# Where a column sum is taken: the mean row of a graph-attention kernel from GpSimd's running sum, adj's buffers on multiples of 512 bytes, and two-input comparisons

## The chip, the cores and the metric

The kernel runs on one core of a Trainium2 chip. The metric is the time of one execution on the device in microseconds; "the time" of a kernel is the median of its runs. A core has five engines with a queue of instructions each: TensorE (PE; its weight loads are listed as PEld), VectorE (DVE), ScalarE (ACT), GpSimd (POOL) and SyncE (SP), which here only issues transfers. ACT and POOL issue transfers too. Sixteen DMA engines carry them out. A wait between engines is a wait on a semaphore. The on-chip memory has 128 partitions; a tile of [128, n] has n elements in each.

## The reference, cut to what matters

Two layers over a graph of N = 4096 nodes with 512 features; about one entry of adj in a thousand is 1, some four neighbours a node. The first layer is attention over the neighbours with eight heads of 64, the second a mean over the neighbours with two dense products. Each is added to its input and normalised.

```python
Wh = jnp.einsum('nf,hfo->hno', x, W)
f1 = jnp.einsum('hno,ho->hn', Wh, a[:, :F_OUT])
f2 = jnp.einsum('hno,ho->hn', Wh, a[:, F_OUT:])
e = jax.nn.leaky_relu(f1[:, :, None] + f2[:, None, :], ALPHA)
e = jnp.where(adj[None, :, :] > 0, e, NEG_INF)
attn = jax.nn.softmax(e, axis=-1)
out = jnp.einsum('hnm,hmo->hno', attn, Wh)
...
mask = (adj > 0).astype(x.dtype)
agg = mask @ x / jnp.maximum(jnp.sum(mask, axis=1, keepdims=True), 1.0)
combined = jnp.concatenate([x @ W_self + b_self, agg @ W_nb + b_nb], axis=-1)
out = jax.nn.relu(combined @ W_comb + b_comb)
...
x = _layernorm(x + out, axis=-1)
```

A node without neighbours has all its scores at the same value, so its softmax is flat, and its row of `out` is the mean of all rows of Wh. This is the "mean row" of the kernel: one row, the average over 4096 nodes.

## The kernel before

The kernel does not multiply by the dense mask. It turns adj into short lists of neighbours and gathers rows by index.

**The adjacency loop** (b = 0 to 26, to about 202 us). Nodes are handled in 32 blocks of 128. For each block of adj, `load_adj` (line 427, SP's queue) brings two halves of 1 MB into the tiles `at` (four buffers); `mask_adj` (L433, ACT) turns a half into bf16 `ab` (three buffers) and counts it; `fold_adj` (L452, PE) packs the mask into key values in PSUM; `max_keys` (L467, DVE) takes the largest keys of a row; and once in four blocks `decode` (L469 to 566, DVE with a few small matmuls) makes the lists of neighbours. It is a generator: the loop takes a few steps of it per block. Two comparisons of `decode`, `va` (L500) and `ni` (L509), work on small tiles; a third, `lt` (L535), is a 128x128 tile for each block, followed by a two-input instruction (L536) that finishes the 0/1 matrix. `late_lists` has the same pair (L594, L595). Blocks 28 to 31 of adj come later, in the attention stage.

In the same loop every node block of x is loaded (`load_x`, SP), transposed on PE (`transposed`, L353) and copied from PSUM to the tile xT by ACT, and then multiplied with the weights: `node_half`, 8 matmuls of 128x264 (L369), whose result of 528 columns DVE copies to a tile `row` (L373, three buffers). The 528 columns are 8 scores f2, 512 of Wh and 8 scores f1. `node_rest` (L396 to L398) copies the scores away on GpSimd, and `store` (L974) writes the row block to the table t0 in HBM, from GpSimd's queue, except for the last block (w = 31), whose store is SP's.

**The mean row** is made from x: the mean of Wh's rows is the mean of x's rows times the weights. For most blocks the copy to xT is done in four pieces with an accumulator each (L361), which sums the columns of x; for four early blocks ACT copies (L356) and DVE reduces (L358). After the loop `mean_row` reduces the sums (L405, L406), multiplies them with the weights `w_sb` (L412, 16 matmuls with one column of weights), copies the result (L416) and stores it as row N + 2 of t0 (L417, ACT's queue).

**After the loop** the order is written by hand. SP issues the last block's store, then the loads of `wr` and `wc` (1 MB each) and two late pieces of adj into `m` (`load_late`). Then comes the first gather, `gather(t0, 0, ...)`: five indirect transfers per block (`rows_of`, L631, GpSimd's queue), four of rows that are shared by several nodes (k = 1 to 4, over the first N + 2 rows) and one over the whole table (k = 0). Its buffer `g` has five copies, `GA` = 5. The first lies where `w_sb` and the sums had been, the others where `at`, `colf`, `ab` and the like had been; so each waits for the last reader of those. Then the folds of adj's blocks 26 and 27 (LB - 1 and LB) and the last decode, the product of W_nb and W_comb (`fold_weights`, PE and ACT), and the attention stage proper (L681 to L755), which runs to about 530 us. The second layer follows.

All tiles are laid out in memory in the order in which they are asked for, so a tile's size moves those behind it. Some tiles ask for more than they use for that reason (`wc` for 8 columns more, `ni` for 8 instead of 4).

Of the kernel before, what the change touches and what calls it, by code (L numbers as in the profile page):

```python
# [31 lines left out]
F32 = mybir.dt.float32  # L32
# [3 lines left out]
AF = mybir.ActivationFunctionType  # L36
OP = mybir.AluOpType
# [3 lines left out]
P = 128  # L41
# [19 lines left out]
G = 4  # L61
# [52 lines left out]
def listed_layers(  # L114
# [207 lines left out]
    def bias_columns(brw):  # L322

        bt = ps.tile([P, 2 * FB], F32, name="sm", bufs=2)
        nc.tensor.transpose(bt, brw, ident[0 : 2 * FB, 0 : 2 * FB])
        bcol = small.tile([P, 2 * FB], F32, name="bcol", bufs=1)
        nc.scalar.copy(bcol, bt)
        return bcol
# [19 lines left out]

    def transposed(b, wp, sums=None):

        tp = ps.tile([P, FB, P], F32, name="tp", bufs=1)
        for c in range(FB):
            nc.tensor.transpose(tp[:, c, :], xs[:, b, ts(c, P)], ident)  # L353
        t = wp.tile([P, FB, P], F32, name="xT", bufs=4)
        if sums is None or b % 2 == 0 and b < XL:
            nc.scalar.copy(t, tp)  # L356
            if sums is not None:
                nc.vector.tensor_reduce(sums[:, :, b : b + 1], tp, AX.X, OP.add)  # L358
        else:
            for c in range(FB):  # L360
                nc.scalar.activation(  # L361
                    t[:, c, :], tp[:, c, :], AF.Copy, accum_out=sums[:, c, b : b + 1]
                )
        return t
# [36 lines left out]

    def mean_row(w_sb, sums, wp):

        xm = small.tile([P, FB], F32, name="xm", bufs=1)
        nc.vector.tensor_reduce(xm, sums, AX.X, OP.add)  # L405
        nc.vector.tensor_scalar(xm, xm, 1.0 / N, None, OP.mult)  # L406
        mr = wp.tile([P, FW], F32, name="row", bufs=3)
        for k in range(2):
            r = slice(k * HW, (k + 1) * HW)
            pq = ps.tile([1, HW], F32, name="sm", bufs=2)  # L410
            for c in range(FB):
                nc.tensor.matmul(  # L412
                    pq, lhsT=xm[:, c : c + 1], rhs=w_sb[:, c, r],
                    start=(c == 0), stop=(c == FB - 1),
                )
            nc.vector.tensor_copy(mr[0:1, r], pq)  # L416
        nc.scalar.dma_start(t0[N + 2 : N + 3, :], mr[0:1, :])  # L417
# [51 lines left out]
    def decode(b0, dp, place):  # L469
# [24 lines left out]
        for g in range(G):  # L494
# [4 lines left out]
        va = dp.tile([P, G, KL], F32, name="va", bufs=1)  # L499
        nc.vector.tensor_scalar(va, nb, float(SHIFT), None, OP.is_ge)  # L500
        nc.vector.tensor_reduce(deg[:, bs], va, AX.X, OP.add)
# [3 lines left out]
        )  # L505
        ni = dp.tile([P, 8], F32, name="ni", bufs=1)[:, 0 : G * K0].rearrange(
            "p (g k) -> p g k", g=G
        )
        nc.vector.tensor_scalar(ni, L[:, :, 0:K0], 0.0, float(N + 2), OP.is_equal, OP.mult)  # L509
# [21 lines left out]
        for b in range(b0, b0 + G):  # L531
            io, off, en = iota[:, 0:P], lst[:, b, KL : KL + 1], end[:, b : b + 1]
            lt = dp.tile([P, P], F32, name="lt", bufs=1)
            st = place(b)
            nc.vector.tensor_scalar(lt, io, en, None, OP.is_lt)  # L535
            nc.vector.scalar_tensor_tensor(st, io, off, lt, OP.is_ge, OP.mult)  # L536
            sts.append(st)
            yield
# [31 lines left out]
    def late_lists(dp, place):  # L570
# [21 lines left out]
        for b in range(NE):  # L592
            lt = dp.tile([P, P], F32, name="lt", bufs=1)
            nc.vector.tensor_scalar(lt, iota[:, 0:P], endl[:, b : b + 1], None, OP.is_lt)  # L594
            nc.vector.scalar_tensor_tensor(  # L595
                place[:, b, :], iota[:, 0:P], tl[:, b, KL : KL + 1], lt, OP.is_ge, OP.mult
            )
            if b % 2:
                yield
# [227 lines left out]
    def weight(pool, name):  # L827
        w = pool.tile([P, FB * HD + (8 if name == "wc" else 0)], F32, name=name)
        return w[:, 0 : FB * HD].rearrange("p (c o) -> p c o", c=FB)
# [7 lines left out]
    bp = bp_cm.__enter__()  # L837
    colf = bp.tile([P, SC], F32, name="colf")
    nc.gpsimd.iota(
        colf, [[1, SC]], base=0, channel_multiplier=0, allow_small_or_imprecise_dtypes=True  # L840
# [28 lines left out]
    nc.scalar.dma_start(brow[0:1, :], b_comb.rearrange("(a o) -> a o", a=1))  # L869
    sums = xa.tile([P, FB, NB], F32, name="sums")  # L870
    pa = []
# [3 lines left out]
    nc.scalar.copy(av[:, 0], pa[0])  # L875
    xT = transposed(0, wp, sums)

# [29 lines left out]
    def node_block(w, xT, between=None, keep=False, then=lambda: None):  # L907
# [11 lines left out]
        if not keep:  # L919
            store(w, row, nc.gpsimd)  # L920
        return row

# [54 lines left out]
    for b in range(LB):  # L977
# [6 lines left out]
        for k in range(2):  # L984
            some(lists)
        ahead = [transposed(w + 1, wp, sums) if w + 1 < NB else None]
        key_bank(b + 1)
        mask_adj(b + 1, 0)

        def then():  # L990
            ahead.append(transposed(w + 2, wp, sums))
            mask_adj(b + 1, 1)
# [21 lines left out]
    loaded = load_fold(1, w_nb, m2, weight(fc, "wc"))  # L1014
    mean_row(w_sb, sums, wp)
    for k in range(2):
# [13 lines left out]
    m2s = fold_weights(loaded, place, "pw")  # L1030
    fold_adj(LB - 1, dp)
    max_keys(LB - 1)
    for k in range(4):
# [588 lines left out]
```

## Time and profile before

| | |
|---|---|
| median of 7 runs | 774.17 us (760.61 to 784.87) |
| the profiled execution | 770.34 us, of which the span from the first to the last instruction is 768.6 us |
| mean granted TensorE clock of the profiled execution | 0.906 |
| instructions | 9452 |
| busy: PE, DVE, ACT, POOL | 599.4, 409.3, 410.6, 353.5 us |
| moved by DMA | 210.46 MB, 274 GB/s over the span |
| the adjacency loop | to about 202 us |
| the attention stage | about 212 to 530 us |
| the second layer | about 530 to 768 us |

The profile is one execution on the chip. A row of a group gives the line, the engine, the operation, the tile written and the tiles read, the shapes and the count; then the busy time, the mean duration of one, and the idle time of the engine just before them with what ended most of it. A timeline's row gives start, duration, engine, line, operation and, in brackets, the idle time before it and its releaser. A "queue" (SPq, ACTq, POOLq) is the issuing of transfers, not the transfer.

### The profile page before, as it was taken

Reading aid. Unit: us, or ns where it says so; the run is one execution under the profiler, and the core shown is the slowest. Engines: PE = TensorE matmul, PEld = TensorE weight load, DVE = VectorE, ACT = ScalarE, POOL = GpSimd, SP = SyncE. Lnnn points to the kernel's source line nnn. Section 1 sums busy time; section 2 is a strip of 40 time slices with the busy share of each in tenths; the row PEclk is TensorE's granted clock in tenths of the full one; section 3 lists DMA queues with packets and bytes.
Section 4 is the critical chain, followed back from the end, with each engine's and each line's share of the span. In section 5 each row is a group of like instructions: output and inputs, shape, how many; then the busy total and the mean of one; then the engine's idle time right before and its main releaser. Section 6 shows DMA issues by size and latency. Waiting matters only on the chain.

```text
span 768.6 us, 9452 instructions
## 1 busy us (share of the span) xinstructions
PE 599.4 (78%) x2569; PEld 294.4 (38%) x2570; DVE 409.3 (53%) x1182; ACT 410.6 (53%) x1087; POOL 353.5 (46%) x472
## 2 busy tenths in 40 slices
PE   6888888899735697669686676868959987888794
PEld 4666666676412343223232232323413322222231
DVE  6246686978573667557675764652024233323342
ACT  3587878888511386566464454444234444434353
POOL 4111211121175456555565564645736666666620
PEclk9799999999867799888798898979989998998998
DMA  8999999999976679887786687658758877787752
GB/s 265 391 374 380 393 395 393 393 394 391 368 219 170 196 273 388 293 249 242 294 237 224 213 243 244 202 183 271 210 180 249 270 237 252 238 269 255 237 204 74
DMA packets 92108, 210.46 MB, mean 274 GB/s; under 512 B 13761, under 2 KB 13769, under 8 KB 92048
## 3 DMA queue, kind: packets, MB, share of 16 engines
q1 hardware_dynamic: 63296, 114.32, 41.2%
q0 software_dynamic: 28560, 95.17, 40.0%
q8 instruction: 23, 0.38, 0.2%
q10 hardware_dynamic: 192, 0.28, 0.1%
q14 instruction: 37, 0.30, 0.1%
HBM read 175.91 MB, written 33.83 MB: 273 GB/s over the span
## 4 chain that ended last, share of the span: by engine, by line
PE 33%; DMA 19%; issue 15%; ACT 12%; another core or an unknown queue 12%; DVE 7%; SPq 1%; ACTq 0%; DVEq 0%
DMA at<-in_adj_dram 18%; PE pw L776 7%; PE nm L776 6%; PE pw L750 6%; ACT ab L433 3%; PE num L706 3%; PE pw L369 3%; PE nm L783 2%; PE pw L783 2%; PE pw L314 1%; ACT xs L736 1%; ACT xs L745 1%; ACT xT L356 1%; PE sm L412 1%
## 5 line engine op out<-in xcount | busy, mean ns | idle before, releaser
L631 POOL DMA_INDIRECT g<-t,idx x290 | 275.5, 950 | 191.4 <-issue 80.3
L750 PE MATMUL pw<-wr,xT 128*128 128x512 f32 x256 | 130.8, 657 | 0.7 <-ACT xT L356 0.7
L433 ACT ACTIVATE ab<-at 128x2048 bf16<-128x2048 int32 x56 | 107.2, 1915 | 41.4 <-DMA at<-in_adj_dram 32.4
L369 PE MATMUL pw<-w_sb,xT 128*128 128x264 f32 x496 | 124.9, 400 | 4.0 <-DVE row L393 2.0
L369 PEld LDWEIGHTS pw<-w_sb,xT 128*128 128x128 f32 x496 | 92.6, 195 | 27.8 <-issue 3.7
L706 PE MATMUL num<-g,own 128*32 128x256 f32 (+1 forms) x512 | 43.0, 463 | 69.4 <-ACT num L699 52.2
L396 POOL COPY lst<-row 128x8 f32<-128x8 f32 x32 | 6.9, 216 | 154.8 <-DVE row L373 118.8
L750 PEld LDWEIGHTS pw<-wr,xT 128*128 128x128 f32 x256 | 51.1, 211 | 70.0 <-issue 64.2
L681 DVE TENSOR_TENSOR g<-g,ew 128x2048 f32<-128x2048 f32 x32 | 73.1, 2284 | 0.0
L776 PE MATMUL pw<-m,xT 128*128 128x512 f32 x128 | 63.1, 620 | 6.6 <-issue 6.2
L776 PE MATMUL nm<-m,xT 128*128 128x512 f32 x128 | 64.3, 643 | 2.7 <-issue 2.7
L714 DVE RECIPROCAL rd<-num 128x8 f32<-128x8 f32 x32 | 6.6, 207 | 93.1 <-PE num L706 21.7
L671 ACT ACTIVATE ew<-e 128x40 f32<-128x40 f32 x32 | 6.6, 207 | 85.8 <-issue 43.6
L706 PEld LDWEIGHTS num<-g,own 128*32 128x32 f32 x512 | 15.0, 122 | 86.8 <-ACT num L699 57.8
L373 DVE COPY row<-pw 128x264 f32<-128x264 f32 x62 | 26.5, 428 | 38.0 <-PE pw L369 31.3
L353 PE MATMUL tp<-ident,xs 128*128 128x128 f32 x256 | 40.4, 282 | 6.9 <-issue 2.0
L754 ACT COPY row<-pw 128x512 f32<-128x512 f32 x32 | 18.7, 584 | 47.9 <-PE pw L750 22.4
L353 PEld LDWEIGHTS tp<-ident,xs 128*128 128x128 f32 x256 | 31.6, 145 | 30.6 <-issue 18.7
L799 DVE SCALAR_TENSOR_TENSOR sm<-g,lst,pw 128x512 f32<-128x512 f32 x15 | 11.3, 754 | 59.1 <-remote 32.3
L799 DVE SCALAR_TENSOR_TENSOR sm<-g,lst,nm 128x512 f32<-128x512 f32 x15 | 11.3, 753 | 59.1 <-PE nm L783 39.2
L776 PEld LDWEIGHTS nm<-m,xT 128*128 128x128 f32 x128 | 25.0, 204 | 42.5 <-issue 38.4
L776 PEld LDWEIGHTS pw<-m,xT 128*128 128x128 f32 x128 | 23.5, 194 | 46.3 <-issue 42.6
(234 smaller groups left out, 964.2 us busy)
## 6 DMA issues: line engine op xcount, KB each, us to landing
at<-in_adj_dram SPq DMA_DIRECT2D x56, 1024.0 KB
xt<-xT SPq DMA_DIRECT2D x32, 256.0 KB
t<-row SPq DMA_DIRECT2D x32, 256.0 KB
xT<-xt SPq DMA_DIRECT2D x32, 256.0 KB
out_dram<-row SPq DMA_DIRECT2D x32, 256.0 KB
t<-row POOLq DMA_DIRECT2D x31, 264.0 KB
xs<-in_x_dram SPq DMA_DIRECT2D x31, 256.0 KB
m<-in_adj_dram SPq DMA_DIRECT2D x10, 512.0 KB
```

The costliest lines, as they stand in the source:

```text
L353: nc.tensor.transpose(tp[:, c, :], xs[:, b, ts(c, P)], ident)
L369: nc.tensor.matmul(pw, lhsT=xT[:, c, :], rhs=w_sb[:, c, k * HW : (k + 1) * HW], start=(c == 0), stop=(c == FB - 1),)
L373: nc.vector.tensor_copy(row[:, k * HW : (k + 1) * HW], pw)
L433: nc.scalar.activation(ab, loads.pop((b, h)), AF.Relu, accum_out=asum[:, b, h : h + 1])
L631: nc.gpsimd.indirect_dma_start(out=out, out_offset=None, in_=table, in_offset=bass.IndirectOffsetOnAxis(ap=at, axis=0),)
L681: nc.vector.tensor_tensor(gv, gv, E[b][:, sl].unsqueeze(3).to_broadcast([P, sl.stop - sl.start, H, D]), OP.mult,)
L706: nc.tensor.matmul(NM[b][ts(k, HP), a * HD : a * HD + r.stop - r.start], lhsT=OWN[b][:, k, :], rhs=G0[b][:, K0 + k, r], start=False, stop= ...
L750: nc.tensor.matmul(pz, lhsT=xT[:, c, :], rhs=m2[:, c, :], start=(c == 0), stop=(c == FB - 1))
L754: nc.scalar.copy(z[:, 0:HD], pz)
L776: nc.tensor.matmul(NM[b], lhsT=xT[:, c, :], rhs=m1[:, c, :], start=False, stop=(c == FB - 1), skip_group_check=True,)
L783: nc.tensor.matmul(NM[b][ts(k, HP), :], lhsT=OWN[b][:, k, :], rhs=g[:, K0 + k, 0:HD], start=False, stop=True, tile_position=(0, k * HP), s ...
L799: nc.vector.scalar_tensor_tensor(yp, Y[b], lst[:, b, KL + 1 : KL + 2], NM[b], OP.mult, OP.add)
```

## The change

Four things change.

1. The sums over x go. `transposed` copies to xT with one ACT instruction for every block, and DVE reduces nothing. In their place `add_row` lets GpSimd keep a running sum `acc` of the rows of Wh: a copy for block 0, then an addition of [128, 528] for blocks 1 to 30, each queued behind that block's store. `mean_row` multiplies `acc` and the last block's `row` by a column of 1/N (`inv_n`) and so sums over the partitions: four matmuls with one column of weights instead of 16.
2. The fold of adj's block 26 and its maxima move ahead of the mean row; before, they stood behind it. The order on PE is then: eight fold matmuls, four of the mean row; on DVE: four maxima, then the two copies of the mean row. ACT's and SP's orders stay as they are.
3. Sizes: `bcol` 16 columns instead of 8, `acc` new with 640, `wc` without its 8 further columns, `xm`, `sums` and `ni` gone (`ni` uses the buffer of `jx`). In the built program the four buffers of `at` start at 141312, 149504, 157696 and 165888 bytes within a partition, multiples of 512; before, they started at 143808, 152000, 160192 and 168384, each 448 past a multiple. `colf`, `acc`, `ab` and the first tiles of `decode` start on multiples of 512 too.
4. The comparisons `va` and `lt` become two-input instructions: compare, then multiply with a tile of ones.

The diff, without repetitions:

```diff
...
         bt = ps.tile([P, 2 * FB], F32, name="sm", bufs=2)
         nc.tensor.transpose(bt, brw, ident[0 : 2 * FB, 0 : 2 * FB])
-        bcol = small.tile([P, 2 * FB], F32, name="bcol", bufs=1)
+        bcol = small.tile([P, 4 * FB], F32, name="bcol", bufs=1)[:, 0 : 2 * FB]
         nc.scalar.copy(bcol, bt)
         return bcol
...
         if b < NB:
             eng.dma_start(xs[:, b, :], x[ts(b, P), :])
-    def transposed(b, wp, sums=None):
+    def transposed(b, wp):
         tp = ps.tile([P, FB, P], F32, name="tp", bufs=1)
         for c in range(FB):
             nc.tensor.transpose(tp[:, c, :], xs[:, b, ts(c, P)], ident)
         t = wp.tile([P, FB, P], F32, name="xT", bufs=4)
-        if sums is None or b % 2 == 0 and b < XL:
-            nc.scalar.copy(t, tp)
-            if sums is not None:
-                nc.vector.tensor_reduce(sums[:, :, b : b + 1], tp, AX.X, OP.add)
-        else:
-            for c in range(FB):
-                nc.scalar.activation(
-                    t[:, c, :], tp[:, c, :], AF.Copy, accum_out=sums[:, c, b : b + 1]
-                )
+        nc.scalar.copy(t, tp)
         return t
     def node_half(b, k, xT, w_sb, row):
...
             f1s[:, b, 0:K0, :], row[:, TW:FW].unsqueeze(1).to_broadcast([P, K0, H])
         )
-    def mean_row(w_sb, sums, wp):
-
-        xm = small.tile([P, FB], F32, name="xm", bufs=1)
-        nc.vector.tensor_reduce(xm, sums, AX.X, OP.add)
-        nc.vector.tensor_scalar(xm, xm, 1.0 / N, None, OP.mult)
+    def add_row(b, row):
+        if b == 0:
+            nc.gpsimd.tensor_copy(acc, row)
+        else:
+            nc.gpsimd.tensor_tensor(acc, acc, row, OP.add)
+
+    def mean_row(row, wp):
+
         mr = wp.tile([P, FW], F32, name="row", bufs=3)
         for k in range(2):
             r = slice(k * HW, (k + 1) * HW)
             pq = ps.tile([1, HW], F32, name="sm", bufs=2)
-            for c in range(FB):
-                nc.tensor.matmul(
-                    pq, lhsT=xm[:, c : c + 1], rhs=w_sb[:, c, r],
-                    start=(c == 0), stop=(c == FB - 1),
-                )
+            for n, t in enumerate((acc, row)):
+                nc.tensor.matmul(pq, lhsT=inv_n, rhs=t[:, r], start=(n == 0), stop=(n == 1))
             nc.vector.tensor_copy(mr[0:1, r], pq)
         nc.scalar.dma_start(t0[N + 2 : N + 3, :], mr[0:1, :])
...
             nc.vector.max(nb[:, g, 8:16], kj[:, g, :])
             yield
         va = dp.tile([P, G, KL], F32, name="va", bufs=1)
-        nc.vector.tensor_scalar(va, nb, float(SHIFT), None, OP.is_ge)
+        nc.vector.scalar_tensor_tensor(
+            va, nb, float(SHIFT), ones[:, 0 : G * KL].rearrange("p (g k) -> p g k", g=G),
+            OP.is_ge, OP.mult,
+        )
         nc.vector.tensor_reduce(deg[:, bs], va, AX.X, OP.add)
         L = lst[:, bs, :]
         nc.vector.scalar_tensor_tensor(
             L[:, :, 0:KL], nb, float(2 - SHIFT), va, OP.add, OP.mult
         )
-        ni = dp.tile([P, 8], F32, name="ni", bufs=1)[:, 0 : G * K0].rearrange(
-            "p (g k) -> p g k", g=G
-        )
+        ni = dp.tile([P, G, KH], F32, name="jx", bufs=1)[:, :, 0:K0]
         nc.vector.tensor_scalar(ni, L[:, :, 0:K0], 0.0, float(N + 2), OP.is_equal, OP.mult)
         nc.vector.scalar_tensor_tensor(
             idx[:, bs, 0:K0], L[:, :, 0:K0], float(N + 1), ni, OP.min, OP.max
...
             io, off, en = iota[:, 0:P], lst[:, b, KL : KL + 1], end[:, b : b + 1]
             lt = dp.tile([P, P], F32, name="lt", bufs=1)
             st = place(b)
-            nc.vector.tensor_scalar(lt, io, en, None, OP.is_lt)
+            nc.vector.scalar_tensor_tensor(lt, io, en, ones, OP.is_lt, OP.mult)
             nc.vector.scalar_tensor_tensor(st, io, off, lt, OP.is_ge, OP.mult)
             sts.append(st)
             yield
...
         nc.vector.tensor_add(endl, tl[:, :, KL], nl)
         for b in range(NE):
             lt = dp.tile([P, P], F32, name="lt", bufs=1)
-            nc.vector.tensor_scalar(lt, iota[:, 0:P], endl[:, b : b + 1], None, OP.is_lt)
+            nc.vector.scalar_tensor_tensor(
+                lt, iota[:, 0:P], endl[:, b : b + 1], ones, OP.is_lt, OP.mult
+            )
             nc.vector.scalar_tensor_tensor(
                 place[:, b, :], iota[:, 0:P], tl[:, b, KL : KL + 1], lt, OP.is_ge, OP.mult
             )
...
     fp = fp_cm.__enter__()
     def weight(pool, name):
-        w = pool.tile([P, FB * HD + (8 if name == "wc" else 0)], F32, name=name)
+        w = pool.tile([P, FB * HD], F32, name=name)
         return w[:, 0 : FB * HD].rearrange("p (c o) -> p c o", c=FB)
     oo_cm = tc.tile_pool(name="owners", bufs=1, side="right")
...
     bp_cm = tc.tile_pool(name="lists", bufs=1, side="right")
     bp = bp_cm.__enter__()
     colf = bp.tile([P, SC], F32, name="colf")
+    acc = bp.tile([P, 5 * P], F32, name="acc")[:, 0:FW]
     nc.gpsimd.iota(
         colf, [[1, SC]], base=0, channel_multiplier=0, allow_small_or_imprecise_dtypes=True
     )
...
         load_x(b)
     nc.vector.memset(brow, 0.0)
     nc.scalar.dma_start(brow[0:1, :], b_comb.rearrange("(a o) -> a o", a=1))
-    sums = xa.tile([P, FB, NB], F32, name="sums")
     pa = []
     for k in range(2):
         pa.append(ps.tile([P, HD], F32, name=("sm", "key")[k], bufs=(2, 1)[k]))
         nc.tensor.matmul(pa[k], lhsT=ones[0:1, :], rhs=av[0:1, k], start=True, stop=True)
     nc.scalar.copy(av[:, 0], pa[0])
...
         node_rest(w, row)
         if not keep:
             store(w, row, nc.gpsimd)
+            add_row(w, row)
         return row
     def on_own(b):
...
             pads(wp)
         for k in range(2):
             some(lists)
-        ahead = [transposed(w + 1, wp, sums) if w + 1 < NB else None]
+        ahead = [transposed(w + 1, wp) if w + 1 < NB else None]
         key_bank(b + 1)
         mask_adj(b + 1, 0)
         def then():
-            ahead.append(transposed(w + 2, wp, sums))
+            ahead.append(transposed(w + 2, wp))
             mask_adj(b + 1, 1)
         if b not in AHEAD:
...
     store(w - 1, row, nc.sync)
     m2 = weight(fp, "wr")
     loaded = load_fold(1, w_nb, m2, weight(fc, "wc"))
-    mean_row(w_sb, sums, wp)
+    fold_adj(LB - 1, dp)
+    max_keys(LB - 1)
+    mean_row(row, wp)
     for k in range(2):
         load_late()
     wc = loaded[1]
...
     gps = [gather_buffer(0)]
     G0[0] = gather(t0, 0, gps[0])
     m2s = fold_weights(loaded, place, "pw")
-    fold_adj(LB - 1, dp)
-    max_keys(LB - 1)
     for k in range(4):
         some(lists)
     fold_adj(LB, dp)
```

More of the change, by code (lines that the diff above doesn't have):

```diff
@@ L875, in listed_layers @@
     nc.scalar.copy(av[:, 0], pa[0])
-    xT = transposed(0, wp, sums)
+    xT = transposed(0, wp)
     def times(eng, a, pr, by):
```

## The prediction

> **What bounds the kernel now.** I read the slices first, then the stretch of the adjacency loop (40 to 200 us) by engine and by DMA queue, then the chain and the timeline where that loop ends. The loop, b = 0 to 26, runs to about 202 us. Three views of it: busy time of each engine between 40 and 200 us (the stretch, its length, then PE, PEld, DVE, ACT, POOL busy, granted clock, DMA share, GB/s); the DMA queues between 60 and 180 us; and who waited for whom between 40 and 200 us (total, times, longest).
>
> ```profile
> 40.00:200.00 160.00, 141.54 (x800) 104.03 (x799) 116.19 (x460) 131.10 (x327) 31.34 (x112) 0.99 1.04 389
> ```
>
> ```profile
> DMA packets 22749, 47.23 MB, mean 394 GB/s; under 512 B 1167, under 2 KB 1167, under 8 KB 22738
> ...
> q1 hardware_dynamic: 21060, 41.43, 92.6%
> q0 software_dynamic: 1678, 5.67, 11.9%
> ```
>
> ```profile
> POOL lst L396 <- DVE row L373: 109.3, 23, 6.9
> ...
> ACT ab L433 <- DMA at<-in_adj_dram: 23.8, 30, 3.6
> DVE row L373 <- PE pw L369: 22.7, 18, 1.9
> ```
>
> The DMA engines are full (92.6 + 11.9% of 16 engines), PE is at 88% (141.5 of 160 us), ACT at 82%, DVE at 73%, POOL at 20%. The mask of ACT waits for adj to land 30 times. The queue's own waits say the opposite too (SP waits for masks to free the four "at" buffers, 85 us in all), but with the engines full there is always another load under way. So the loop goes at the pace of its bytes, and a shorter ACT or DVE is not a shorter loop.
>
> The end of the loop is different. The timeline from 190 to 232 us, in rows cut to the ones that matter, and one row of the timeline from 232 to 290 us:
>
> ```profile
> 202.16 0.34 SPq L974 DMA_DIRECT2D t<-row  x1
> 203.11 1.91 ACT L433 ACTIVATE ab<-at 128x2048 bf16<-128x2048 int32 x1 [1.09 <-DMA at<-in_adj_dram]
> 204.75 6.19 PE L412 MATMUL sm<-w_sb,xm 128*1 128x264 f32 x14 [3.08 <-DVE xm L406]
> 211.91 1.91 ACT L433 ACTIVATE ab<-at 128x2048 bf16<-128x2048 int32 x1 [6.80 <-PE sm L412]
> 212.23 1.03 POOL L631 DMA_INDIRECT g<-t,idx  x1 [9.07 <-PE sm L412]
> 213.56 0.98 POOL L631 DMA_INDIRECT g<-t,idx  x1 [0.31 <-issue]
> ```
>
> ```profile
> 251.16 0.94 POOL L631 DMA_INDIRECT g<-t,idx  x1 [7.64 <-issue]
> ```
>
> The first gather and the last mask both wait for the mean row's matmuls (L412). From 212.23 us GpSimd then issues 25 gathers back to back, one every 1.25 us, up to 243.5 us; that run is the start of the attention stage, and the chain of waits goes through its landings.
>
> **The change, part by part.** Durations are from the groups by form:
>
> ```profile
> L361 ACT ACTIVATE xT<-tp 128x128 f32<-128x128 f32 x112 | 29.1, 274 | 9.8 <-PE tp L353 9.8
> L361 ACT ACTIVATION_READ_ACCUMULATOR xT<-tp 128x1 f32 x112 | 23.1, 207 | 0.0
> L356 ACT COPY xT<-tp 128x512 f32<-128x512 f32 x36 | 21.2, 588 | 0.3 <-remote 0.2
> L879 POOL TENSOR_TENSOR xs<-w_sb,xs 128x1024 f32<-128x1024 f32 x2 | 4.7, 2358 | 3.2 <-ACT xs L875 3.2
> ```
>
> *ACT and DVE lose the sums.* 28 blocks go from four copies with accumulators, 4 x (0.274 + 0.207) = 1.92 us, to one copy of 0.588: 28 x 1.34 = 37 us less ACT work. Four reductions of 0.69 us (L358), and L405 and L406, leave DVE. All of it lies beside a full DMA: 0 on the path. The loop has one hole, between 50 and 60 us, where the packet records of the trace fill only 93 and then 76% of the engines; if ACT made that, 1.5 us come back. Several masks there wait for their own loads, so I take 0.
>
> *GpSimd gains one copy and 30 adds of 528 columns.* By the 1024-column row an add is 2358 x 528/1024 = 1.22 us; with a fixed part like the small copies' (0.19 us) 1.3 us: 31 x 1.25 = 39 us. Behind each add on GpSimd's queue stand the next block's three copies and its store to t0 (L974), for which nothing waits before the gathers; GpSimd has 109 us of waiting for DVE to put it in. The row buffer is held some 1.3 us longer, with three buffers and 5.9 us a block. 0 on the path, if DVE is not held by it. It can be: the copies of L397 take 185 ns in the middle and 630 at most, L535 on DVE 286 and 529, so the two engines do stop each other. DVE's decode has some 8 us per four blocks of two-input or one-input SBUF work, about 30% of its time; an add that meets it costs perhaps 0.3 us, 31 x 0.3 = 9 us spread over a DVE with 27% to spare. Bounds: 0 to 1.25 us an add; I take 0, as DVE's copies of the rows from PSUM (L373, 414 to 434 ns over 62) show no stop at all.
>
> The Trainium skill ("SBUF — State Buffer", Who interferes with whom) says that a DVE instruction with two SBUF inputs and a GpSimd instruction that reads SBUF shut each other out for the whole instruction. That speaks against both the adds and the two-input comparisons; by an estimate from it each add would hold DVE for all its 1.25 us, 39 us in all, which still leaves DVE under the loop's 160 (116 + 39 = 155).
>
> *The comparisons.* L535 and L594 (38) go from 286 ns towards the 351 of L536, which has the same tile and two inputs: 38 x 0.065 = 2.5 us, 30 of them under the loop; the other eight cost 0.5 us at most on a DVE that is 60% busy. L500 and L509 are as small. 0.
>
> *adj's buffers.* In the built program the four "at" buffers start at 448 past a multiple of 512 bytes, and at 0 in the changed one. Does that change the packets' time? Loads of wr and wc (also 448; 206 to 212 us, 99.8% of 16 engines, 1145 packets) come to 83.7 ns a packet; in the packet records the middle of all 2 KB packets is 84 ns, for x (128), for xT (64) and for adj (448) alike. None starts at 0. Bounds: 0, or, if all 56 x 512 = 28,672 packets went at the 81 ns that the fastest per cent takes instead of the 87.9 that they average between 60 and 180 us (92.6% of 1920 us, less the small ones, over 20,230), 28,672 x 6.9/16 = 12.4 us. I take 0, the value of three offsets out of three. A loss has no reason: each power of two that divides 448 divides 0.
>
> The Trainium skill ("DMA: Bandwidth & Descriptors", How a descriptor splits into AXI transactions) charges a start off a 256-byte boundary with the bytes before it: 192 bytes, six beats on 64. By an estimate from it the loads, 149 us at 394 GB/s, would lose 6/70, and the sum would be some 13 us lower; the equal 84 ns at three offsets say no.
>
> *The mean row leaves the path.* 16 matmuls on w_sb become four on acc and the last row, placed after the fold of block 26 (two fold matmuls of 32x512 per strip). The first gather's buffer lies over w_sb, whose last reader is now the last block's matmul, done at 201.7. What is late next? The gather reads t0, so it needs the last store (L974, issued at 202.16, its last packet at 206.5). Between the mean's last matmul (211.4) and the gather (212.23) lie 0.8 us; after the store I allow 0.5: the first gather at 207.0, 5.2 us earlier. Its fifth part needs the mean row itself: the fold of block 26 no longer waits behind L412 and ends about 202.5, the row matmuls end about 204.5, DVE copies them after its two places and four maxima at about 206, and the store lands about 2 us later; the fifth gather is issued at 207 + 4 x 1.25 = 212. The last mask no longer waits for PE (207 instead of 213.8), so the last decode ends some 8 us earlier than 226. The run of 25 gathers ends at 238.3. The loads of wr, wc and m, which fill the DMA until 214 us, now share it with the first five or six gathers: their 1.6 MB are 4 us at 394 GB/s, and the fold that needs wc starts only at 230. From 251 us on gathers follow the freeing of buffers by earlier blocks, so the shift stays. I take -5.2 us; bounds 0 (the shared DMA swallows it) and -8 (decode and mask set the start).
>
> **Sum.** The profiled execution took 770.3 us (span 768.6 and 1.7 around it): 770.3 - 5.2 = 765.1. The middle of seven runs is 774.2, from 760.6 to 784.9, so the same step from there is **769**. Two per cent, 15.5 us, is about what a measurement of this kernel can tell from no change.
>
> **Rivals.** (1) *Alignment pays.* The packets of adj drop to 81 ns: -5.2 - 12.4, **757**. For it: adj is 58.7 of the loop's 76.8 MB, and the loop is bound by nothing else. Against it: the equal 84 ns. (2) *The adds hold DVE, and slow PE.* PE is free 18.5 us of 160, or 0.68 us for each of the 27 blocks there, and it waits for DVE's copies of the rows. If each add keeps DVE from the row copy for its full 1.25 us and GpSimd's own stretching adds as much again as L397's worst (0.45), 31 x (1.70 - 0.68) = 32 us, of which half meet a decode: +16 on the loop, +11 in all, **785**; if all meet one, 801. It decides from 0.68 us an add on. Against it: L373 never stretched, and 30 of the DVE waits there are for PE, not the reverse. (3) *The early gathers gain nothing,* since the DMA is full until 214 us, and the stage's start follows DVE and ACT: **774**.
>
> **How the numbers follow.** Forecast 0.50, alignment 0.22, ports 0.13, nothing 0.15. Faster by over 2% is under 758.7: most of the alignment case and the forecast's edge with runs that scatter by 1%, 0.20. Slower by over 2% is above 789.7: the upper half of the ports case, 0.09. Within: 0.71. The range 755 to 782 leaves out the lower edge of alignment and the upper part of ports; the forecast's own is 764 to 774.
>
> **What would show it.** GpSimd's first gather at about 207 instead of 212.23 us, with a wait for the store of t0 and none for PE; its 25th before 240; the last mask not waiting for PE. ACT at about 68% and the DMA as full as before in the loop, its GB/s at 394; over 405 would be alignment. DVE's share of the loop under 80%, L373 at 432 ns. Wrong if the loop ends after 204 us (ports), or at 196 or before (alignment), or if the 25th gather still ends at 243.

## The result and the profile after

| | before | changed |
|---|---|---|
| median of the runs | 775.68 us (758.92 to 796.74, 63 runs) | 773.02 us (765.84 to 781.46, 26 runs) |
| profiled execution | 770.34 us, span 768.6 | 775.76 us, span 774.1 |
| last row store issued (end of the loop) | 202.16 us | 205.83 us |
| first gather issued | 212.23 us | 209.39 us |
| from the first gather to the end of the span | 556.4 us | 564.7 us |

The ratio of record, changed to before, is 1.0079 with the interval [1.0041, 1.0117]: the same within 2%. Its sign is opposite to that of the medians (773.02/775.68 = 0.997), because the ratio compares only the runs within 1.5% of each kernel's fastest (12 of 63 and 19 of 26), and the fastest of 63 lies lower (758.92 against 765.84 us). So the sign has to come from the stages and from further runs. The profile has the loop end 3.7 us later, and the first gather 2.8 us earlier.

The loop first: two stretches of the kernel before, then the changed kernel's busy times between 40 and 200 us and its stretches 60 to 140, 140 to 180 and 180 to 200 us (the stretch, its length, PE, PEld, DVE, ACT, POOL busy with their counts, granted clock, DMA share, GB/s).

```profile
60.00:140.00 80.00, 69.98 (x395) 51.16 (x391) 58.31 (x234) 64.14 (x160) 14.35 (x52) 0.98 1.05 394
140.00:180.00 40.00, 36.50 (x216) 27.04 (x215) 32.15 (x135) 33.87 (x87) 7.78 (x28) 1.00 1.05 393
```

```profile
40.00:200.00 160.00, 142.92 (x789) 103.23 (x787) 131.97 (x447) 117.53 (x144) 66.84 (x135) 0.97 1.03 388
...
60.00:140.00 80.00, 68.74 (x377) 49.42 (x376) 65.76 (x221) 57.85 (x71) 31.92 (x65) 0.98 1.05 408
140.00:180.00 40.00, 36.00 (x204) 25.90 (x202) 35.30 (x124) 28.56 (x36) 16.12 (x35) 0.96 0.97 347
180.00:200.00 20.00, 18.39 (x109) 13.05 (x101) 19.00 (x66) 16.80 (x21) 8.85 (x16) 1.00 1.04 397
```

Over the whole stretch nothing has changed: 388 GB/s against 389. Divided, two opposite things have. From 60 to 140 us the loads run at 408 GB/s with the same full engines (394 before). Then the DMA is no longer full, at 347 GB/s and a share of 0.97 instead of 1.05, and DVE nearly is: 35.3 of 40 us, then 19.0 of 20. In the whole stretch DVE has 132 us instead of 116, though it lost reductions. Who waited for whom between 40 and 200 us, before and then changed:

```profile
PEld pw L369 <- DVE row L373: 3.3, 4, 1.7
...
PE pw L369 <- DVE row L373: 2.0, 2, 1.4
```

```profile
ACT ab L425 <- DMA at<-in_adj_dram: 20.3, 23, 2.8
ACT xT L355 <- PE tp L353: 15.9, 8, 6.0
...
PEld pw L361 <- DVE row L365: 11.6, 12, 2.0
PE pw L361 <- DVE row L365: 8.4, 9, 1.5
```

PE's waits for DVE's row copies, 3.3 and 2.0 us before, are 11.6 and 8.4. ACT waits for PE in its turn, up to 6 us at once, so the masks that free the buffers of adj come late. The cause shows in the groups by form (mean ns of one is the last number before the second bar), before and then changed, and in the changed kernel's timeline at 158 us:

```profile
L535 DVE TENSOR_SCALAR lt<-iota,end 128x128 f32<-128x128 f32 x22 | 6.2, 284 | 0.6
...
L558 DVE TENSOR_SCALAR idx<-jx 128x16 uint32<-128x16 f32 x5 | 0.9, 174 | 0.2
```

```profile
L528 DVE SCALAR_TENSOR_TENSOR lt<-iota,end,ones 128x128 f32<-128x128 f32 x20 | 13.3, 667 | 0.5
L492 DVE SCALAR_TENSOR_TENSOR va<-nb,ones 128x64 f32<-128x64 f32 x6 | 9.5, 1588 | 0.2
...
L551 DVE TENSOR_SCALAR idx<-jx 128x16 uint32<-128x16 f32 x5 | 2.6, 515 | 0.2
...
L398 POOL TENSOR_TENSOR acc<-acc,row 128x528 f32<-128x528 f32 x30 | 39.6, 1320 | 0.7
```

```profile
157.20 0.34 DVE L528 SCALAR_TENSOR_TENSOR lt<-iota,end,ones 128x128 f32<-128x128 f32 x1
...
157.96 1.63 DVE L528 SCALAR_TENSOR_TENSOR lt<-iota,end,ones 128x128 f32<-128x128 f32 x1
158.11 1.32 POOL L398 TENSOR_TENSOR acc<-acc,row 128x528 f32<-128x528 f32 x1
...
160.02 0.35 DVE L528 SCALAR_TENSOR_TENSOR lt<-iota,end,ones 128x128 f32<-128x128 f32 x1
```

The same instruction takes 0.34 us, 1.63 us and 0.35 us; the long one ends just after the add (159.59 and 159.43). Before, va took 196 ns on the mean; here all six meet an add. The add itself, with 1.32 us, takes no longer than the mean of all 30.

At the end of the loop, the timeline of the changed kernel from 204 to 210 us, cut to the rows that matter:

```profile
205.66 1.91 ACT L425 ACTIVATE ab<-at 128x2048 bf16<-128x2048 int32 x1 [2.51 <-PE key L444]
...
205.83 0.34 SPq L970 DMA_DIRECT2D t<-row  x1
...
206.74 0.61 PE L407 MATMUL sm<-row,inv_n 128*1 128x264 f32 x2
...
209.39 1.24 POOL L626 DMA_INDIRECT g<-t,idx  x1 [2.50 <-issue]
```

The last mask waits 2.5 us, for the fold of block 26, instead of 6.8 us for the mean row. The mean row's matmuls are done 2 us before the first gather, which follows the last store by 3.6 us instead of 10.1. The profile names nothing that this gather waited for. In the packet records of the trace the last of the store's 128 packets ends at 207.56 us, 1.8 us before the gather.

### The profile page after: what moved, and what is told of

It is laid out like the page before. It is cut to its first block, busy times and chain, and to the rows that moved or that the text cites. A ratio compares the mean times of both kernels' runs of the same rounds, so it can differ in the third digit from the quotient of the medians.

```text
span 774.1 us, 9265 instructions
## 1 busy us (share of the span) xinstructions
PE 600.3 (78%) x2561; PEld 294.2 (38%) x2562; DVE 427.7 (55%) x1176; ACT 396.0 (51%) x891; POOL 395.2 (51%) x503
## 4 chain that ended last, share of the span: by engine, by line
PE 43%; issue 15%; DVE 13%; DMA 13%; ACT 9%; another core or an unknown queue 4%; SPq 1%; POOL 0%; ACTq 0%; DVEq 0%
DMA at<-in_adj_dram 11%; PE nm L771 8%; PE pw L771 8%; PE pw L745 7%; PE num L701 3%; PE nm L778 3%; PE pw L361 3%; PE pw L778 3%; PE pw L314 2%; PE tp L314 2%; ACT ab L425 2%; ACT xs L731 1%; DVE row L365 1%; ACT xT L355 1%
## 5 line engine op out<-in xcount | busy, mean ns | idle before, releaser
L745 PE MATMUL pw<-wr,xT 128*128 128x512 f32 x256 | 132.8, 666 | 1.5 <-ACT xT L355 1.5
L361 PE MATMUL pw<-w_sb,xT 128*128 128x264 f32 x496 | 127.0, 403 | 8.8 <-DVE row L365 8.8
L425 ACT ACTIVATE ab<-at 128x2048 bf16<-128x2048 int32 x56 | 106.8, 1908 | 40.1 <-DMA at<-in_adj_dram 35.3
L355 ACT COPY xT<-tp 128x512 f32<-128x512 f32 x64 | 37.3, 582 | 18.5 <-PE tp L353 15.9
L626 POOL DMA_INDIRECT g<-t,idxe x30 | 28.4, 948 | 24.9 <-issue 8.2
```

The costliest lines, as they stand in the source:

```text
L361: nc.tensor.matmul(pw, lhsT=xT[:, c, :], rhs=w_sb[:, c, k * HW : (k + 1) * HW], start=(c == 0), stop=(c == FB - 1),)
L425: nc.scalar.activation(ab, loads.pop((b, h)), AF.Relu, accum_out=asum[:, b, h : h + 1])
L626: nc.gpsimd.indirect_dma_start(out=out, out_offset=None, in_=table, in_offset=bass.IndirectOffsetOnAxis(ap=at, axis=0),)
L745: nc.tensor.matmul(pz, lhsT=xT[:, c, :], rhs=m2[:, c, :], start=(c == 0), stop=(c == FB - 1))
```

## The experiments

The theory after the first profile: faster loads (alignment) and an earlier gather (mean row) are paid back by the adds, which keep DVE from what it has to read from SBUF. Four kernels take the change apart.

**e1: alignment alone.**

```diff
-    colf = bp.tile([P, SC], F32, name="colf")
+    colf = bp.tile([P, SC + 112], F32, name="colf")[:, 0:SC]
```

> The kernel before with one edit: colf gets 112 more columns that nothing uses, so that the four buffers of adj start on multiples of 512 bytes (448 past one before). Theory (alignment makes the packets faster): the loop moves about 408 GB/s between 60 and 140 us instead of 393, 4% of some 160 us, so the last row store is issued at about 196 us instead of 202.2, the first gather at about 206 instead of 212.2, and the ratio to the kernel before is about 0.992. Rival (the 408 GB/s of the changed kernel came from the shorter ACT work): 393 GB/s, the last store at 202, ratio 1.000.

Ratio 0.9918 [0.9881, 0.9955], as expected. Its stretches, and its timeline's last store and first gather:

```profile
60.00:140.00 80.00, 73.75 (x420) 54.78 (x418) 62.39 (x250) 68.22 (x175) 15.19 (x56) 0.98 1.05 408
140.00:180.00 40.00, 37.49 (x219) 27.44 (x218) 32.89 (x138) 35.24 (x87) 8.64 (x30) 1.00 1.05 409
```

```profile
195.83 0.34 SPq L974 DMA_DIRECT2D t<-row  x1
...
204.67 1.02 POOL L631 DMA_INDIRECT g<-t,idx  x1 [7.85 <-PE sm L412]
```

With all of ACT's sums in place the loads run at 408 GB/s to 180 us, and the loop ends 6.3 us earlier. Less ACT work is not what made them faster. The edit moves the buffers of adj, and leaves the masks `ab` where they were, at 448.

**e2: the changed kernel without the alignment.**

```diff
-    acc = bp.tile([P, 5 * P], F32, name="acc")[:, 0:FW]
+    acc = bp.tile([P, FW], F32, name="acc")
```

> The changed kernel with acc at 528 instead of 640 columns, which puts the buffers of adj back at 448 past a multiple of 512; all else as changed. Theory: 393 GB/s between 60 and 140 us instead of 408; the adds still hold DVE; the last store at 207 to 212 us instead of 205.8; ratio to the kernel before 1.010 to 1.015. Rival (alignment does nothing): 408 GB/s and 206 us.

Ratio 0.9975 [0.9929, 1.0021], not the 1.010 to 1.015 expected. The loads are at 393 GB/s, as expected; but the last store is at 205.34 us, not 207 or later. With the adds where the change puts them DVE is the bound, and the speed of the loads hardly matters: the loop ends at 205.3 us unaligned, and at 205.8 and 203.8 aligned (the change, and once more in e5).

**e3: no adds.**

```diff
-        else:
-            nc.gpsimd.tensor_tensor(acc, acc, row, OP.add)
```

> The changed kernel without the 30 additions on GpSimd (acc is only the copy of block 0, so the mean row is left without blocks 1 to 30). Theory (the adds hold DVE's instructions that read SBUF, about 20 us in the loop, and DVE paces the loop from 140 us on): DVE is busy about 18 us less between 20 and 205 us, va takes about 0.22 us and lt 0.35, the loads stay at 408 GB/s to 180 us, the last store is issued at about 197 us and the first gather at about 201; ratio to the kernel before about 0.988. Rival (the loop is late because of ACT's single copy to xT or of the order on PE): the last store at 205 as in the changed kernel, with DVE shorter and idle.

Ratio 0.984 [0.979, 0.9891]. Groups by form and stretches:

```profile
L526 DVE SCALAR_TENSOR_TENSOR lt<-iota,end,ones 128x128 f32<-128x128 f32 x24 | 8.4, 348 | 0.6
...
L490 DVE SCALAR_TENSOR_TENSOR va<-nb,ones 128x64 f32<-128x64 f32 x6 | 1.3, 225 | 0.2
```

```profile
60.00:140.00 80.00, 70.77 (x411) 51.98 (x408) 61.98 (x240) 59.74 (x73) 15.87 (x56) 1.00 1.05 408
140.00:180.00 40.00, 37.05 (x216) 27.63 (x213) 32.94 (x135) 31.52 (x39) 8.02 (x28) 1.00 1.05 408
```

va falls from 1588 to 225 ns, lt from 667 to 348. The last store is at 195.02, the first gather at 200.40. By these means the adds held lt for 20 x 0.319 = 6.4 us, va for 8.2, idx for 1.7, and two other pairs (kk with top, jk with iota) for 2.6: 19 us of DVE, or 0.63 us an add, and the loop is 10.8 us longer for it. Over the same 482 instructions, from 20 us to the last store, DVE is busy 123.4 us instead of 142.1: 18.6 us less, about the 18 that were expected. (Between 20 and 205 us it is only 8.9 us less, as this kernel is ahead and does more there.)

**e4: the same adds, moved.** The add of a block waits for the first half of the next block's row, and runs beside key maxima and the second row copy.

```diff
...
             node_half(w, 0, xT, w_sb, row)
+            nc.gpsimd.tensor_copy(f2s[:, w, :], row[:, 0:H])
+            add_row(*done.pop())
             if between is not None:
...
             store(w, row, nc.gpsimd)
-            add_row(w, row)
+            done.append((w, row))
```

> The changed kernel with the same 30 additions, each one block later: GpSimd waits for the first half of the next block's row, and adds while DVE takes key maxima and copies the second half from PSUM, with no two-input instruction queued in between. Theory (what costs is what the add meets on DVE): va about 0.22 us and lt about 0.35 in the mean, DVE held under 4 us in all, the last store at about 197 us, the first gather at about 201, ratio to the kernel before about 0.988. Rival (what costs is GpSimd's time or the row buffers that it holds, which are now held longer): the last store at 206 us or later, ratio 1.008 or more.

Ratio 0.9746 [0.9678, 0.9814], better than the 0.988 expected; the same kernel once more (e12) gave 0.9822. GpSimd does all the work of the change, and little is held by it. Its timeline at 164 us:

```profile
163.71 0.88 DVE L460 MAX8 kk<-key 128x8 f32<-128x128 f32 x4
...
163.86 0.18 POOL L911 COPY f2s<-row 128x8 f32<-128x8 f32 x1 [4.46 <-DVE row L365]
...
164.01 1.30 POOL L399 TENSOR_TENSOR acc<-acc,row 128x528 f32<-128x528 f32 x1
...
164.50 0.42 DVE L365 COPY row<-pw 128x264 f32<-128x264 f32 x1
...
164.84 0.70 DVE L480 TENSOR_SCALAR ke<-kk 128x384 int32<-128x384 int32 x1
```

Maxima (0.88 us for four) and the copy from PSUM (0.42) run their usual time under the add; only the tail of it still meets an instruction of one SBUF input (0.70 instead of 0.35). va is back at 225 ns, lt at 348, the last store at 194.64, the first gather at 200.31. The rival, that row buffers are held too long, falls.

**e5 to e8** took 630 to 638 us, and the kernel before beside them 641.14 (639.09 to 642.95): the loop ends within some 2 us of where it does in the other runs, the time behind the first gather is shorter by more than 120 us and steadier. **e5** is the changed kernel itself.

> The changed kernel once more, unedited, for the scatter of what lies behind the loop. Theory (the loop's end is a property of the kernel, the length from the first gather to the end scatters by some 10 us from one execution to the next): the last store again at 205 to 206 us and the first gather at 209 to 210; from there to the end between 552 and 566 us, as the six profiles so far; ratio to the kernel before between 0.998 and 1.010. Rival (the change itself makes the later stages longer, the 564.7 us of its first profile): 563 us or more again.

Ratio 0.9953 [0.9934, 0.9971], below the range expected, and 3.2 us less in the medians. The last store is at 203.80, the first gather at 207.42, each 2 us earlier than in the first profile, and 428 us follow, not 552 to 566. The rival, that the change makes the later stages longer, falls: the ratio is below 1, and among the executions of some 770 us the length behind the first gather went from 552.1 (e2) to 565.7 us (e1), in kernels that do the same there.

**e6: one-input comparisons, adds as changed.**

```diff
-        nc.vector.scalar_tensor_tensor(
-            va, nb, float(SHIFT), ones[:, 0 : G * KL].rearrange("p (g k) -> p g k", g=G),
-            OP.is_ge, OP.mult,
-        )
+        nc.vector.tensor_scalar(va, nb, float(SHIFT), None, OP.is_ge)
...
-            nc.vector.scalar_tensor_tensor(lt, io, en, ones, OP.is_lt, OP.mult)
+            nc.vector.tensor_scalar(lt, io, en, None, OP.is_lt)
...
```

> The changed kernel with the comparisons in their one-input forms of before; the adds stay. Theory (an add keeps out one-input instructions that read and write SBUF as well, as it did the small idx of the decode, 515 ns instead of 174): va and the first lt that meet an add still take about 1.6 us, the last store at 204 to 206 us, ratio 1.000 to 1.008. Rival (only the second input contends): va about 0.2 us, lt 0.29 in the mean, DVE about 15 us less busy between 20 and 205 us, the last store at 198 to 200.

```profile
L525 DVE TENSOR_SCALAR lt<-iota,end 128x128 f32<-128x128 f32 x22 | 12.6, 572 | 0.6
L492 DVE TENSOR_SCALAR va<-nb 128x64 f32<-128x64 f32 x6 | 9.3, 1548 | 0.2
```

The groups by form have va at 1548 ns and lt at 572: the one-input form is held as well. The last store is at 203.16, a little before the 204 to 206 expected; the ratio, 0.9935 [0.9909, 0.9962], is not told apart from e5's. The form of the comparison is not the fault; what is beside it is.

**e7: adj at 256 past a multiple of 512** (e1's edit with 48 columns instead of 112), and **e10: at 128** (80 columns).

> The kernel before with 48 unused columns behind colf, so that the buffers of adj start 256 past a multiple of 512 bytes. If a multiple of 512 is needed: 393 GB/s, packets as before (a third of them longer than 84 ns), the last store at 202 us. If 256 is enough: 408 GB/s, the last store at 196, ratio 0.992. Anything between would say that the cost grows with the distance from a boundary.

> The kernel before with 80 unused columns behind colf, so that the buffers of adj start 128 past a multiple of 512 bytes, as x's do. If what counts is a multiple of 256: 393 GB/s, the last store at 201 to 202 us, ratio 1.000, and packets longer than 84 ns as before. If 128 is enough (x's packets, which start at 128, are not long beside an adj that starts at 0 or 256): 408 GB/s, the last store at 195, ratio 0.990.

e7: ratio 0.9903 [0.9884, 0.9923], last store 194.81. e10: 0.9999 [0.9941, 1.0056], last store 201.08. What was measured of the 2 KB packets of the loads (adj's and x's together; the records do not say which is which) between 70 and 150 us, from the packet records of the traces:

| adj starts at (bytes past a multiple of 512) | kernel | longer than 84 ns | mean | GB/s, 60 to 140 us |
|---|---|---|---|---|
| 448 | before | 60.4% | 87.6 ns | 394 |
| 128 | e10 | 60.8% | 87.4 ns | 396 |
| 256 | e7 | 0.2% | 84.2 ns | 408 |
| 0 | e1 | 0.2% | 84.2 ns | 408 |

For adj a multiple of 256 is enough, and between 128 and 448 there is no gradation. x, at 128 in all four, is an eighth of these bytes; with 0.2% of all packets long it can't be slow.

**e8: e4 with the mean row ahead of the fold of block 26,** the order of before.

> The kernel of e4 (adds between the copies) with the mean row back ahead of the fold of block 26 and its maxima, as the kernel before has it. Theory (what takes the mean row off the path is that it needs four short matmuls that wait for no DVE reduction, not the order): the last store at 195 us, the first gather at 200 to 201, ratio within 0.003 of e4. Rival (the order is what counts): the first gather 2 to 4 us later, at 203 or 204.

Ratio 0.9836 [0.9812, 0.986], last store 195.28, first gather 200.56, 5.3 us after the store (5.7 in e4). The ratio is not within 0.003 of e4's 0.9746, but it is of e12's 0.9822, the same kernel. The order counts for nothing here; the sum that has been formed beside the loop is what takes the mean row off the path.

e5, e7 and e8 stand beside the same runs of the kernel before, and these scatter by less than 1%. So they show in whole times what the parts are worth: the alignment alone 0.9903 (e7), with the new mean row and adds that hold little 0.9836 (e8), with the adds where the change puts them 0.9953 (e5). In microseconds of 641 that is -6.2, -4.3 and +7.5, together -3.0. The intervals of the three do not overlap.

**e9, e11, e12** ran beside e10. e9 is the kernel before, e12 is e4, e11 is e4 with e6's comparisons.

> The kernel before, unedited, for its stage times on the chip of the day. Theory: 393 GB/s between 60 and 180 us, the last store at 201 to 202 us, the first gather 10 us later at 211 to 212, so that the changed kernel's gain is what its first gather gains (207.4 against about 211.5) and nothing behind it; ratio 1.000.

> The kernel of e4 (adds between the copies) with the one-input comparisons of before. Theory (they are 65 ns shorter each, and meet no add in either form): DVE about 2 us less busy between 20 and 205 us than in e4, the last store at 194.5 to 195.5 us, the time within 0.3% of e4. Rival (the one-input form takes the port for itself and holds the moved adds): adds longer than 1.30 us in the mean, the last store at 196 or later.

> The kernel of e4 once more, to stand beside e9 to e11. The last store at 194 to 196 us, the first gather at 200 to 201; the ratio to the kernel before by the difference of the first gathers, 11 us: 0.983 where the time is about 640 us, 0.986 where it is about 775.

e9: last store 202.45, first gather 211.04, close to what was expected; ratio to itself 1.0054 [1.0, 1.0109]. So among runs that scatter like these an identical kernel can come out half a per cent slower, which is most of the 1.0079 of record. e12: 0.9822 [0.9728, 0.9915], last store 195.06, first gather 200.22. e11: 0.9826 [0.9726, 0.9926], last store 195.46, adds of 1296 ns, as in e4: no difference between the forms that these runs can tell. Its small va and idx take 244 and 212 ns, against 196 and 174 in the kernel before, so a few are probably still held.

**e13 and e14** ask why x, which starts at 128 in every kernel but e14, was a wrong witness. e13 sets the pieces of adj's buffers apart, e14 is e4 with x's tile at 0.

```diff
-            at = loads[b, h] = ap.tile([P, NG // NH, SC], I32, name="at", bufs=4)
+            at = loads[b, h] = ap.tile([P, NG // NH, SC + 64], I32, name="at", bufs=4)[:, :, 0:SC]
```

> The kernel before with 64 unused columns behind each 512-column piece of adj's buffers: they still start 448 past a multiple of 512, and every 2 KB packet still starts off a multiple of 256 (448 or 192 past one of 512), but no two packets share a unit of 256 bytes. Theory A (two neighbouring packets share a unit of 256 bytes, and wait for each other; x's packets lie one to a partition and have no neighbour in flight): 408 GB/s between 60 and 140 us, under 2% of the packets longer than 84 ns, the last store at 195 to 196 us, ratio 0.990 to 0.993. Theory B (the start of each packet counts, whatever lies beside it): 393 GB/s, about 60% of the packets longer, the last store at 201 to 202.5, ratio 1.000.

> The kernel of e4 with x's tile moved from 128 past a multiple of 512 bytes to a multiple (by unused columns; the tiles behind it stay where they were, modulo 512). Theory A and the packet records so far (x at 128 is not slow beside an aligned adj): the last store at 194.6 to 195.3 us as in e4 and e12, the ratio 0.982 to 0.984. Theory B with x counted in: x is an eighth of the loop's packets, 4% of an eighth of 160 us is 0.8 us, the last store at 194 us.

e13: 0.9983 [0.9913, 1.0053], 394 GB/s, 61.3% of the packets longer than 84 ns, last store 201.59. That neighbours share a unit of 256 bytes is not the reason: theory A falls. e14: 0.9783 [0.9668, 0.9897], last store 194.91, packets as in e1 (0.2%, 84.2 ns): x at 0 gains nothing, since x at 128 lost nothing. Why adj's packets mind their start and x's do not stays open.

## Why the prediction was wrong

**The sum.** The first gather (last store in brackets) gives the account: before 212.2 (202.2); aligned 204.7 (195.8), -7.5; the sum made without ACT and DVE and its adds left out 200.4 (195.0), -4.3; the adds where the change puts them 209.4 (205.8), +9.0. Together -2.8 us. These are single profiles: the same kernels again gave 211.0 (e9, before) and 207.4 (e5, changed), so each step is good to some 2 us. The prediction had 0, -5.2 and 0. That its sum came within 2.4 us of this is luck: two of its terms were wrong, and cancelled. Where the runs are steady the kernel gained 3.2 of 641 us (e5). The ratio of record says 0.8% slower; the control e9 says how little that sign is worth.

**"Alignment: I take 0, the value of three offsets out of three": failed.** The term was 6.3 us at the end of the loop (e1). The middle of the packet times was the wrong statistic. It is 84 ns over the whole execution, but 86 ns in the loop between 70 and 150 us, where most packets are adj's. 84 ns is the commonest value at every offset, and the cost lies in the other 60%, which stretch to 98 ns. The prediction had the mean, 87.9 ns, in its hand and used it only for a bound, against 81 ns, which almost no packet of the loop reaches (the fastest per cent of them takes 84); against 84.2 the same sum is 28,672 x (87.6 - 84.2)/16 = 6.1 us. The loads of wr and wc are not affected (between 206 and 212 us 7% of the packets are longer than 84 ns, at 448 too), nor are x's: two witnesses that could not see it. Rival 1 was right in its mechanism and twice too large. The rule of the Trainium skill ("DMA: Bandwidth & Descriptors", How a descriptor splits into AXI transactions), which charges a start off a 256-byte boundary, names the right boundary for adj: 0 and 256 are fast, 128 and 448 slow (e1, e7, e10). The size that the beats give is not borne out (four per cent, where by an estimate from the page it would be nine), and x at 128 and wr and wc at 448 show no such cost.

**"L373 shows no stop at all", adds at 0: failed.** L373 reads PSUM; it shows no stop in the changed kernel either (433 ns for the seven that run beside an add, 424 for the others). The instructions that stop are those whose inputs lie in SBUF, and these were the ones that the prediction itself had seen stretched (L535, 286 to 529 ns). It set the cost of an add that meets one at "perhaps 0.3 us"; an add holds such an instruction to its own end, for up to 1.45 us (kk with top, 1.75 instead of 0.29). Per add that is 0.63 us on the mean (e3), 19 us in all.

**"27% to spare": failed.** The room was counted over the stretch. DVE copies rows between steps of the decode, and PE waits for these copies longer than before (the waits above). Between 40 and 200 us DVE has 82% (132 of 160 us), but from 140 us on 88 and then 95%, and there the loads fall from 408 to 347 GB/s: a mean over the loop hides where the room ends. Rival 2, the adds that slow PE, is what happened. It had the adds hold the row copy, where they hold the decode ahead of it, and sized the loop's loss at 16 us, where it is 10.8 against e3. By its own point of decision, 0.68 us an add, the 0.63 measured would have cost nothing: it spread PE's free time evenly too. The Trainium skill ("SBUF — State Buffer", Who interferes with whom) was right as far as these runs go. It says that a DVE instruction with two SBUF inputs contends with a GpSimd instruction that reads SBUF; beside an add lt took 1.63 us instead of 0.35. It says that copies and one-input comparisons can contend too; the one-input lt took 1.56 us instead of 0.28 (e6), and in the changed kernel a copy of 12 columns within SBUF (esl) 772 ns instead of 173. It says that reductions never do on this chip; four beside an add took their usual 403 ns. The estimate from it, 39 us, is twice the 19 because half of the adds' time holds nothing.

**Comparisons: the size held.** lt takes 348 ns without adds against 284, the 65 ns of the forecast; and the form makes no difference that these runs can tell (e5 with e6, e12 with e11).

**"37 us less ACT work": mis-sized; that it lies on no path held.** Over the span ACT has 396.0 us instead of 410.6, 14.6 less. The term added 207 ns for each accumulator read to 274 ns of copy, but in the timeline before the four copies of a block start 0.25 us apart (101.44, 101.69, 101.94, 102.19): the reads overlap with the copies. The error cost nothing, as e1, with all the old ACT work, is as fast to 180 us as e3.

**The mean row, -5.2: held in its mechanism, partly in size.** It is -4.3 us from e1 to e3. The prediction had the gather wait for the last store next, and gave it 0.5 us after the store's last packet. In all ten profiles with the new sum it comes 1.5 to 1.9 us after that packet (changed 207.56 and 209.39, e4 198.54 and 200.31), and with the old sum 2.9 to 5.8 us after it. This fits a wait for the store, which no run tested by itself. The gap from the last store's issue to the first gather was 7.2 to 10.1 us with the old sum, and 3.6 or 5.2 to 5.7 with the new one. The two values go with the store: its last packet ends 1.7 us after its issue where the adds have slowed the loop, 3.4 to 3.9 us where they have not. The last mask no longer waits for the mean row. The 25th gather was issued at 240.5 us, 242.6 before: 2.1 us of the first gather's 2.8 were still there. The run of 25 ended at 241.4 us, where the forecast had 238.3. Rival 3, that early gathers gain nothing, falls: from e1 to e3 the 25th is 4.4 us earlier, like the first.

**What it gave as signs of being wrong** worked: 408 GB/s is "over 405", the loop ended after 204 us, and DVE's share passed 80%. Of the signs of being right, ACT came to 73% of the loop, not 68, the first gather to 209.4 us, not 207, and the 25th to 240.5, not under 240. The two signs of the two rivals came together, which the forecast had not provided for: it weighed them as alternatives, and they are parts of one sum.

## What to carry to other kernels

Ask of a witness whether it could have seen the cost: a copy from PSUM says nothing of a conflict in SBUF, and a commonest packet time says nothing of a tail; means over the stretch that matters do. Look at what stands beside work that is moved to GpSimd: the same 30 adds cost 10.8 us at the end of the loop beside comparisons and other work on SBUF, and nothing beside copies from PSUM and maxima (e4, e8, e12, 1.6 to 2.5% faster than before). Try the buffers of a load-bound loop on multiples of 256 bytes: here it was worth 6 us. And add up the parts of a change before choosing among them.

## What the runs showed of the hardware

- An add on GpSimd of 128x528 (1.30 to 1.32 us) holds many DVE instructions that read SBUF until the add ends: the lt at 157.96 us took 1.63 us instead of 0.35, the small idx of 16 columns 515 ns on the mean instead of 174. Not touched, in the changed kernel beside an add, were row copies from PSUM (433 ns), maxima over SBUF (243 and 261), a reduction (403), and a two-input instruction with its second input in PSUM (jk, 403).
- In the records the held DVE instruction begins before the add (157.96 against 158.11 us) and still ends after it. Which of the two asked first can't be read from the starts.
- 2 KB packets that start at 0 or 256 past a multiple of 512 bytes took 84.2 ns on the mean, at 128 or 448 87.4 to 87.6 ns, in the loop's loads, by where adj started. x's packets at 128 were not long beside an aligned adj, and of those between 206 and 212 us in the kernel before, for wr and wc at 448, only 7% were. The reason wasn't found.
- The changed kernel took 773 us in one set of runs and 638 us in another, with the first gather at 209.4 and 207.4 us. Nearly the whole difference lies behind it, where rows are gathered: from the first gather to the end 564.7 us and 428.3 us, at granted clocks of 0.906 and 0.972 (means over the whole execution). The short runs, e5 to e8, all come from one chip, which none of the other experiments used; whether the chip made the difference wasn't tried.
